# Attention weights summed over runs of four key tiles before their product with ones, and the last MLP's first weight loads written ahead of the residual stream's

## The chip, the cores and the metric

The kernel runs on one core of a Trainium2 chip. The core's engines work side by side, each with its own queue of instructions: TensorE (PE, matrix products; its weight loads are shown as PEld), VectorE (DVE), ScalarE (ACT), GpSimd (POOL) and SyncE (SP), on whose queue this kernel issues all of its transfers. They are kept in step by semaphores. The metric is the device time of one execution in microseconds: 3082.72 us is the median of three runs before the change (3080.58, 3082.72 and 3085.39).

## The reference

Two transformer layers in float32 on an input of 2 sequences x 1024 tokens x 512 features. Each layer adds an attention and an MLP, both on a layer norm, to the residual stream:

```python
x = x + _L0_attn_ref(_layernorm(x))   # gated delta rule, 6 heads of 64
x = x + _L0_ffn_ref(_layernorm(x))    # MLP, 4-bit weights, 512 -> 4096 -> 512
x = x + _L1_attn_ref(_layernorm(x))   # latent attention, 16 heads
x = x + _L1_ffn_ref(_layernorm(x))    # MLP, SiLU gate, 512 -> 2048 -> 512, two of every four kept
```

The change touches the third line and the passage into the fourth. The latent attention computes, for each of 16 heads (16 features for queries and keys, 32 for values),

```python
attn = jnp.einsum('bqhd,bkhd->bhqk', q, k) * scale
attn = jax.nn.softmax(attn, axis=-1)
out = jnp.einsum('bhqk,bkhd->bqhd', attn, v)
```

and multiplies the result by `wo`. The last MLP computes `silu(x @ w_gate) * (x @ w_up)`, keeps the two largest of each four in magnitude, and multiplies by `w_down`.

## The kernel before, in words

**The order of parts.** The work is laid out so that a part bound by small operations is woven with a part that keeps PE busy. `weave` (L157) takes steps from a main generator and, for each amount of time that it yields, takes filler steps of another. Three such weaves follow each other: the delta rule of sequence 1 beside the first MLP of sequence 0; the latent attention of sequence 0 beside the first MLP of sequence 1; and, the third part, `third()` (L2125), the latent attention of sequence 1 beside the last MLP of sequence 0 (`Sparse`, L1822). After that stands the last MLP of sequence 1 alone (`Sevens`, L1961), whose products are done with seven block products in place of eight, on sums of weight blocks that were made earlier and kept in HBM (`sums`). For PE, DVE, ACT and POOL the instructions are issued in the order in which the program writes them. SP's order is set by a scheduler.

**A value stage.** In `Latent.run` (L1461) queries are taken in two blocks of 512. For each block a score stage finds the largest score of every query, and a value stage, `values` (L1602), computes the weights again with keys as rows and sums the values. A value stage walks over 32 units: four groups of four heads, and in each group eight key tiles of 128 keys. In loop step `u` (L1703) it does:

- `weights(u)` (L1608): four matmuls, one for each head, to `st_ps` in PSUM; they lie in four row groups of the array and run side by side. ACT takes the exponential into two `es` tiles of 128 x 2 x 512, one for two heads; they come from a pool of eight.
- `gather(u - 1)` (L1639): four matmuls, in four column groups, add `es` times the values to `av_ps`.
- The sum of the exponentials over all keys, which divides the result. It goes through a product with a matrix of ones to `den_ps`, accumulated over the key tiles of a group. In the third part, for odd `u`, `pair(u)` (L1654) first adds the exponentials of key tile `u` onto those of `u - 1`: heads 0 to 2 on POOL, head 3 on DVE. Two steps later `total(u - 2)` (L1661) multiplies that pair's sum by ones, four matmuls.
- After the last key tile of a group, `oT` and `dn` are copied from PSUM, and `divide` (L1697) does four reciprocals and four products on DVE, up to three in a step.

An add onto `es[u - 1]` overwrites what `gather(u - 1)` reads, so POOL and DVE wait for that `av_ps` group. ACT writes a new `es` tile only where all readers of the one four units before are done. In the third part `per_value` is 0 (this is what `alone` stands for), so the weave hands out no steps of the MLP beside it during a value stage. In the second part (`running`) the sums go another way, on DVE alone, and the change leaves that as it is.

**The passage to the last MLP.** When the attention of sequence 1 is done, `third()` takes room for the residual stream of that sequence, `x_last`, and issues its eight loads (L2133). The rest of the MLP of sequence 0 follows. Then `Sevens` is constructed: it opens its pools and writes four sums of token blocks on DVE (`tokens`, L1972). Its `run` (L2024) issues the loads of the first two units of weights (`z_left`, each of three blocks of `w_gate` or `w_up` and one of `sums`), and starts.

Of the kernel before, what the change touches and what calls it, by code (L numbers as in the profile page):

```python
# [26 lines left out]
F32 = mybir.dt.float32  # L27
# [1384 lines left out]
class Latent:  # L1412
# [48 lines left out]
    def run(self, b, side, parked, out, per_score, per_value, running, beside=None, xT=None):  # L1461
# [140 lines left out]
        def values(q2, oT):  # L1602
# [5 lines left out]
            def weights(u):  # L1608
                gr, kt = units[u]
                tiles = [spot() for _ in range(2)]  # L1610
                for h4 in range(4):
                    r = 32 * h4
                    nc.tensor.matmul(  # L1613
                        tiles[h4 // 2][h4 % 2],
                        kT[r : r + CR, gr, kt * P : (kt + 1) * P],
                        q2[r : r + CR, gr, :],
                        start=True,
                        stop=True,
                    )
                es[u] = []  # L1620
                for tile in tiles:
                    t = two.tile([P, 2, QB], F32, tag="es", bufs=8 if alone else 6, name="es")
                    if len(tile) == 3:
                        nc.scalar.activation(t.rearrange("p i q -> p (i q)"), tile[2], AF.Exp, scale=HALF**-0.5)  # L1624
                    else:
                        for i in range(2):
                            nc.scalar.activation(t[:, i, :], tile[i], AF.Exp, scale=HALF**-0.5)
                    es[u].append(t)
# [22 lines left out]
                if kt == TT - 1:  # L1651
                    nc.vector.tensor_copy(oT[:, gr, :], av.pop(gr))

            def pair(u):  # L1654

                for h4 in range(4):
                    t = es[u - 1][h4 // 2][:, h4 % 2, :]
                    eng = nc.vector if alone and h4 == 3 else nc.gpsimd
                    eng.tensor_add(t, t, es[u][h4 // 2][:, h4 % 2, :])  # L1659

            def total(u):  # L1661
                gr, kt = units[u]
                if kt == 1:
                    den[gr] = banks.acc.tile([P, QB], F32, tag="den", name="den_ps")
                for h4 in range(4):
                    nc.tensor.matmul(  # L1666
                        den[gr][32 * h4 : 32 * h4 + 32, :],
                        self.ones,
                        es[u - 1][h4 // 2][:, h4 % 2, :],
                        start=(kt == 1),  # L1670
                        stop=(kt == TT - 1),
                    )
                if kt == TT - 1:
                    dn = two.tile([P, QB], F32, tag="dn", bufs=1, name="dn")
                    nc.vector.tensor_copy(dn, den.pop(gr))
                    for q in range(QT):
                        late.append(lambda q=q: divide(gr, q * P, dn, dn[:, q * P : (q + 1) * P]))
# [25 lines left out]
            for u in range(len(units) + 3):  # L1703
                if u < len(units):
                    weights(u)
                if 0 <= u - 1 < len(units):
                    gather(u - 1)
                if running:
                    if 0 <= u - 1 < len(units):
                        add(u - 1)  # L1710
                    if u > TT and u % TT == 1:
                        total_run(u // TT - 1)
                elif u % 2:
                    if u < len(units):
                        pair(u)
                    if u >= 3:
                        total(u - 2)
                yield per_value
                for _ in range(min(3, len(late))):
                    late.popleft()()  # L1720
# [240 lines left out]
class Sevens(Seven):  # L1961
# [3 lines left out]

    def __init__(self, core, banks, factors, xT, x, b, out):
        super().__init__(core, banks, AF.Silu, core.nc.vector)
        self.factors, self.x, self.b, self.out = factors, x, b, out
        self.wp = core.pools("z_w", 2)
        self.tmp = core.pools("z_tmp", 2)  # L1970
        self.one = core.pools("z_one")
        self.tokens(xT, self.one, core.nc.vector)  # L1972

    def close(self):
        self.core.pools.close("z_one", "z_tmp", "z_w")
# [46 lines left out]
            self.jobs.extend(((c, q), f) for f in calls)  # L2022

    def run(self):  # L2024
        self.left, wds = {}, {}
        todo = [(c, pair, w) for c in range(NC1) for pair in range(2) for w in ("gate", "up")]
        ws = {u: self.weights(u) for u in todo[:2]}

        def hidden(c):
            h = self.tmp.tile([P, 4, 2, T // 2], F32, tag="z_h", bufs=3, name="z_h")  # L2030
# [29 lines left out]
def two_layers(ctx, tc, a):  # L2060
# [25 lines left out]
    with tc.manual_schedule(engines={ENG.PE, ENG.DVE, ENG.Activation, ENG.Pool}):  # L2086
# [38 lines left out]
        def third():  # L2125
            xT = pools("xT_3").tile([P, KC, T], F32, name="xT3")
            done.append(xT)
            yield from att.run(1, None, parks[0], parks[1], 3.4, 0, False, xT=xT)
            x = pools("x3").tile([P, TT, DM], F32, name="x_last")
            held.append(x)  # L2130
            for n in range(TT, NT):
                core.x[n] = x[:, n - TT, :]
                nc.sync.dma_start(out=core.x[n], in_=parks[1][n])  # L2133

        held = []
        weave(third(), sparse.run(0, done[0], a["out"]))
        sparse.close()
        pools.close("xT_2", "x2", "l_w")

        sevens = Sevens(core, banks, factors, done[1], held[0], 1, a["out"])  # L2140
        sevens.run()
        sevens.close()
        pools.close("x3", "xT_3")


# [65 lines left out]
```

## Time and profile before

| | us |
|---|---|
| median of three runs | 3082.72 |
| lowest and highest run | 3080.58 and 3085.39 |
| the profiled execution | 3085.38 |
| its span in the trace | 3083.6 |
| PE busy | 3011.3 |
| DVE busy | 1909.1 |
| ACT busy | 960.7 |
| POOL busy | 695.6 |
| POOL's `es` adds (L1659), 96 | 132.6 |
| DVE's `es` adds (L1659), 32 | 41.3 |
| first value stage of the third part, from 2362.3 | 87.8 |
| second value stage of the third part, from 2640.8 | 95.3 |

Each of the 12652 matmuls counted is one of two records that one float32 product leaves. Matmuls that share the array run side by side, so the mean duration of one record (592 ns for `den_ps`) is not what a group of four products adds to PE's time: a group leaves eight records, and its length is read from the timeline. The granted clock of PE is 1.00 of full speed nearly everywhere; some short stretches have 0.50, and one of them covers 2645 to 2655 us, near the start of the second value stage.

### The profile page before, as it was taken

What the parts mean: (1) busy time and instruction counts of PE and PEld (TensorE: products, weight loads), DVE (VectorE), ACT (ScalarE), POOL (GpSimd) and SP (SyncE); (2) the same over time, 40 slices, a digit from 0 to 9 for tenths busy, and PEclk for the clock granted to TensorE, in tenths of its full rate; (3) what the DMA queues carried; (4) which work ended last, traced back from release to release, by engine and by line L of the source; (5) the groups of instructions that cost most, each with busy time, mean ns of one, the idle gap of its engine ahead of it and who ended that gap; (6) DMA issues with size and microseconds to landing.
All of it is one profiled execution on the core that took longest, in us unless ns stands there. A gap on an engine that the chain in (4) does not pass through costs nothing.

```text
span 3083.6 us, 35160 instructions
## 1 busy us (share of the span) xinstructions
PE 3011.3 (98%) x12652; PEld 1581.9 (51%) x12652; DVE 1909.1 (62%) x3554; ACT 960.7 (31%) x1488; POOL 695.6 (23%) x772
## 2 busy tenths in 40 slices
PE   7999999999999999999999999999999999999999
PEld 6777754555555554645435444446433243234547
DVE  6788733566666544477567656745675577364767
ACT  6554411222222211211462125522113510532221
POOL 3223102122222212464211221222002600440000
PEclk9999999999999999999999999999999999999999
DMA  4222313233232225155111110141010010025211
GB/s 139 66 82 69 90 55 110 67 98 101 96 96 80 90 93 171 58 190 194 36 50 64 52 62 26 36 147 59 24 41 1 32 52 14 1 75 164 72 48 52
DMA packets 196525, 235.36 MB, mean 76 GB/s; under 512 B 53952, under 2 KB 148672, under 8 KB 195840
## 3 DMA queue, kind: packets, MB, share of 16 engines
q1 hardware_dynamic: 196352, 233.12, 23.5%
q8 instruction: 100, 1.64, 0.2%
q14 instruction: 73, 0.60, 0.1%
HBM read 160.42 MB, written 72.61 MB: 76 GB/s over the span
## 4 chain that ended last, share of the span: by engine, by line
PE 81%; DVE 9%; DMA 2%; POOL 2%; issue 2%; ACT 1%; SPq 1%; DVEq 0%; POOLq 0%; ACTq 0%
PE z_ps L1042 24%; PE o_ps L201 12%; PE z_ps L1088 8%; PE u_ps L201 5%; PE g_ps L201 5%; PE st_ps L1613 5%; PE av_ps L1644 4%; PE s_ps L1555 4%; DVE cv L475 2%; DMA sums<-factor 1%; PE proj_ps L201 1%; DVE prod L617 1%; PE wide_ps L654 1%; PE small_ps L644 1%; PE den_ps L1666 1%
## 5 line engine op out<-in xcount | busy, mean ns | idle before, releaser
L1015 ACT COPY part<-z_ps 128x512 f32<-128x512 f32 x288 | 168.4, 585 | 712.8 <-PE z_ps L1042 506.0
L1042 PE MATMUL z_ps<-xT,z_left 128*128 128x512 f32 x768 | 361.1, 600 | 2.5 <-DMA z_left<-in_w_gate 2.4
L1564 DVE TENSOR_REDUCE top<-s_ps 128x2 f32<-128x1024 f32 x256 | 301.0, 1217 | 78.4 <-PE s_ps L1555 78.3
L1042 PE MATMUL z_ps<-xt,z_left 128*128 128x512 f32 x576 | 274.1, 598 | 1.2 <-DVE z_h L1060 1.0
L1624 ACT ACTIVATE es<-st_ps 128x1024 f32<-128x1024 f32 x214 | 209.9, 1023 | 126.0 <-PE st_ps L1613 120.8
L1042 PEld LDWEIGHTS z_ps<-xT,z_left 128*128 128x128 f32 x768 | 142.0, 191 | 189.7 <-issue 162.9
L201 PE MATMUL o_ps<-w_down,h 128*128 128x512 f32 x512 | 230.0, 598 | 0.6 <-DVE part L1076 0.6
L1042 PE MATMUL z_ps<-xT,w_left 128*128 128x512 f32 x384 | 179.5, 596 | 5.5 <-DVE h L1060 2.6
L1076 DVE TENSOR_TENSOR part<-z_ps,part 128x512 f32<-128x512 f32 x108 | 74.4, 689 | 178.6 <-PE z_ps L1042 172.9
L1042 PEld LDWEIGHTS z_ps<-xt,z_left 128*128 128x128 f32 x576 | 106.1, 190 | 145.5 <-issue 122.0
L1659 POOL TENSOR_TENSOR es<-es 128x512 f32<-128x512 f32 x96 | 132.6, 1408 | 143.8 <-PE av_ps L1644 140.1
L1613 PE MATMUL st_ps<-q,kT 17*128 17x512 f32 x1024 | 160.3, 649 | 1.7 <-ACT es L1624 1.7
L1555 PE MATMUL s_ps<-kT,q 16*128 16x512 f32 x1024 | 154.3, 640 | 4.6 <-DVE top L1564 4.6
L201 PEld LDWEIGHTS o_ps<-w_down,h 128*128 128x128 f32 x512 | 94.8, 191 | 108.1 <-issue 103.9
L201 PE MATMUL proj_ps<-xT,wqkv 128*128 128x256 f32 x576 | 133.1, 385 | 7.9 <-ACT raw L459 5.6
L1644 PE MATMUL av_ps<-es,v 128*32 128x512 f32 x1024 | 139.3, 615 | 0.0
L1042 PE MATMUL z_ps<-xt,w_left 128*128 128x512 f32 x288 | 136.4, 596 | 1.6 <-DVE part L1076 1.6
L1686 DVE TENSOR_TENSOR acc<-acc,es 128x1024 f32<-128x1024 f32 x96 | 130.6, 1408 | 0.0
L1077 POOL TENSOR_TENSOR h<-h,part 128x512 f32<-128x512 f32 x48 | 66.3, 1384 | 281.0 <-DVE part L1076 281.0
L1060 DVE TENSOR_TENSOR h<-z_ps,part 128x512 f32<-128x512 f32 x84 | 57.9, 689 | 103.7 <-PE z_ps L1042 91.4
L201 PEld LDWEIGHTS proj_ps<-xT,wqkv 128*128 128x128 f32 x576 | 108.0, 192 | 26.0 <-ACT raw L459 7.7
L1207 DVE TENSOR_TENSOR x<-x,o_ps 128x512 f32<-128x512 f32 x64 | 43.8, 684 | 120.0 <-PE o_ps L201 119.7
(317 smaller groups left out, 5167.3 us busy)
## 6 DMA issues: line engine op xcount, KB each, us to landing
sums<-factor SPq DMA_DIRECT2D x24, 512.0 KB, 3.2
kept_gate<-w_left SPq DMA_DIRECT2D x12, 896.0 KB, 3.8
kept_up<-w_left SPq DMA_DIRECT2D x12, 896.0 KB, 3.8
z_left<-kept_gate SPq DMA_DIRECT2D x12, 896.0 KB, 4.6
z_left<-kept_up SPq DMA_DIRECT2D x12, 896.0 KB, 4.5
wd<-kept_down SPq DMA_DIRECT2D x16, 512.0 KB, 4.5
xl<-park SPq DMA_DIRECT2D x32, 256.0 KB, 3.4
z_left<-sums SPq DMA_DIRECT2D x16, 512.0 KB, 4.1
```

The costliest lines, as they stand in the source:

```text
L201: nc.tensor.matmul(ps, lhsT, rhs, start=(i == 0), stop=(i == len(pairs) - 1))
L1015: self.core.nc.scalar.copy(t, src)
L1042: self.core.nc.tensor.matmul(ps, left[l][:, k, :], self.right[r][:, k, :], start=(first and k == 0), stop=(k == 1), skip_group_check=True,)
L1076: nc.vector.tensor_add(v, ps, v)
L1088: nc.tensor.matmul(ps[:, i * dm : (i + 1) * dm], left[l][:, k, i * P : (i + 1) * P], right[r][k], start=(first and i == 0 and k == 0), sto ...
L1555: nc.tensor.matmul(tiles[h4 // 2][:, h4 % 2 * 512 : h4 % 2 * 512 + 512], q1s[t][r : r + HALF, gr, :], kT[r : r + HALF, gr, j * 512 : (j + ...
L1564: nc.vector.tensor_reduce(top[:, j, h : h + 2], tiles[e].rearrange("p (i k) -> p i k", i=2), AX.X, ALU.max, negate=True)
L1613: nc.tensor.matmul(tiles[h4 // 2][h4 % 2], kT[r : r + CR, gr, kt * P : (kt + 1) * P], q2[r : r + CR, gr, :], start=True, stop=True,)
L1624: nc.scalar.activation(t.rearrange("p i q -> p (i q)"), tile[2], AF.Exp, scale=HALF**-0.5)
L1644: nc.tensor.matmul(av[gr][32 * h4 : 32 * h4 + 32, :], v[:, kt, 4 * gr + h4, :], es[u][h4 // 2][:, h4 % 2, :], start=(kt == 0), stop=(kt == ...
L1659: eng.tensor_add(t, t, es[u][h4 // 2][:, h4 % 2, :])
L1686: nc.vector.tensor_add(t, es[u - 1][e] if kt == 1 else t, es[u][e])
```

## The change

In the value stages of the third part, the exponentials of a run of four key tiles are summed on: each key tile but the first of a run is added onto the one before it, in place, so the fourth holds the sum of all four. `onto(u - 1)` does this in every loop step, and three steps later, once in four, `total(u - 3)` multiplies the fourth tile by ones. Which engines add which heads stays as it was. The pool of `es` tiles has ten in place of eight, which is five key tiles.

The second part moves two statements. `Sevens` is constructed in `third()`, between the making of the tile `x_last` and the issue of its loads; its constructor now issues the loads of the first two weight units, and the opening of the two other pools and the token sums have gone to the start of `run`.

```diff
-                    t = two.tile([P, 2, QB], F32, tag="es", bufs=8 if alone else 6, name="es")
+                    t = two.tile([P, 2, QB], F32, tag="es", bufs=10 if alone else 6, name="es")
...
-            def pair(u):
-
-                for h4 in range(4):
-                    t = es[u - 1][h4 // 2][:, h4 % 2, :]
-                    eng = nc.vector if alone and h4 == 3 else nc.gpsimd
-                    eng.tensor_add(t, t, es[u][h4 // 2][:, h4 % 2, :])
+            def onto(u):
+
+                if u % 4:
+                    for h4 in range(4):
+                        t, v = (es[i][h4 // 2][:, h4 % 2, :] for i in (u, u - 1))
+                        (nc.vector if h4 == 3 else nc.gpsimd).tensor_add(t, t, v)
 
             def total(u):
                 gr, kt = units[u]
-                if kt == 1:
+                if kt == 3:
                     den[gr] = banks.acc.tile([P, QB], F32, tag="den", name="den_ps")
                 for h4 in range(4):
                     nc.tensor.matmul(
                         den[gr][32 * h4 : 32 * h4 + 32, :],
                         self.ones,
-                        es[u - 1][h4 // 2][:, h4 % 2, :],
-                        start=(kt == 1),
+                        es[u][h4 // 2][:, h4 % 2, :],
+                        start=(kt == 3),
                         stop=(kt == TT - 1),
                     )
...
-                elif u % 2:
-                    if u < len(units):
-                        pair(u)
-                    if u >= 3:
-                        total(u - 2)
+                else:
+                    if 0 <= u - 1 < len(units):
+                        onto(u - 1)
+                    if u >= 6 and (u - 3) % 4 == 3:
+                        total(u - 3)
                 yield per_value
...
     def __init__(self, core, banks, factors, xT, x, b, out):
         super().__init__(core, banks, AF.Silu, core.nc.vector)
-        self.factors, self.x, self.b, self.out = factors, x, b, out
+        self.factors, self.x, self.b, self.out, self.xT = factors, x, b, out, xT
         self.wp = core.pools("z_w", 2)
-        self.tmp = core.pools("z_tmp", 2)
-        self.one = core.pools("z_one")
-        self.tokens(xT, self.one, core.nc.vector)
+        self.todo = [(c, pair, w) for c in range(NC1) for pair in range(2) for w in ("gate", "up")]
+        self.ws = {u: self.weights(u) for u in self.todo[:2]}
...
     def run(self):
-        self.left, wds = {}, {}
-        todo = [(c, pair, w) for c in range(NC1) for pair in range(2) for w in ("gate", "up")]
-        ws = {u: self.weights(u) for u in todo[:2]}
+        self.tmp = self.core.pools("z_tmp", 2)
+        self.one = self.core.pools("z_one")
+        self.tokens(self.xT, self.one, self.core.nc.vector)
+        self.left, wds, todo, ws = {}, {}, self.todo, self.ws
...
             x = pools("x3").tile([P, TT, DM], F32, name="x_last")
-            held.append(x)
+            sevens.append(Sevens(core, banks, factors, done[1], x, 1, a["out"]))
             for n in range(TT, NT):
                 core.x[n] = x[:, n - TT, :]
                 nc.sync.dma_start(out=core.x[n], in_=parks[1][n])
```

More of the change, by code (lines that the diff above doesn't have):

```diff
@@ L2133, in third @@
                 nc.sync.dma_start(out=core.x[n], in_=parks[1][n])
-        held = []
+        sevens = []
         weave(third(), sparse.run(0, done[0], a["out"]))
@@ L2138, in two_layers @@
         pools.close("xT_2", "x2", "l_w")
-        sevens = Sevens(core, banks, factors, done[1], held[0], 1, a["out"])
-        sevens.run()
-        sevens.close()
+        sevens[0].run()
+        sevens[0].close()
         pools.close("x3", "xT_3")
```

## The prediction

> **What bounds the kernel now.** The page's first part comes first:
>
> ```profile
> PE 3011.3 (98%) x12652; PEld 1581.9 (51%) x12652; DVE 1909.1 (62%) x3554; ACT 960.7 (31%) x1488; POOL 695.6 (23%) x772
> ```
>
> TensorE (PE) is busy nearly always, and POOL looks idle. That average says nothing about the two stretches that the change touches, the value stages of the third part. I found their ends in the timeline (first `st_ps` product to the first product after the last `den_ps` product) and cut them out with the table of busy times by stretch, together with one run of four key tiles inside the first:
>
> ```profile
> 2362.30:2450.10 87.80, 86.81 (x641) 24.18 (x640) 41.53 (x48) 64.14 (x86) 66.33 (x48) 1.00 0.00 1
> 2640.80:2736.10 95.30, 92.98 (x641) 24.72 (x640) 42.74 (x48) 65.44 (x87) 66.28 (x48) 0.93 0.00 1
> 2393.00:2403.50 10.50, 10.50 (x84) 2.96 (x80) 4.98 (x6) 7.91 (x11) 8.15 (x7) 1.00 0.01 2
> ```
>
> The columns after the length are PE, PEld, DVE, ACT, POOL, then the granted clock. In these stages POOL is busy 66.3 us of 87.8, three times its share of the whole. Four key tiles take 10.5 us, and POOL's six adds take about 8.2 of them. So PE is first, POOL a close second. The timeline of one pair of key tiles shows how they mesh:
>
> ```profile
> 2397.68 4.19 POOL L1659 TENSOR_TENSOR es<-es 128x512 f32<-128x512 f32 x3 [1.29 <-PE av_ps L1644]
> ...
> 2398.31 1.14 PE L1613 MATMUL st_ps<-q,kT 17*128 17x512 f32 x8
> 2398.38 1.12 DVE L1659 TENSOR_TENSOR es<-es 128x512 f32<-128x512 f32 x1 [1.45 <-ACT es L1624]
> ...
> 2399.38 1.06 PE L1644 MATMUL av_ps<-es,v 128*32 128x512 f32 x8
> ...
> 2400.38 1.39 PE L1613 MATMUL st_ps<-q,kT 17*128 17x512 f32 x8
> ...
> 2401.70 1.06 PE L1644 MATMUL av_ps<-es,v 128*32 128x512 f32 x8
> ...
> 2402.58 1.04 PE L1666 MATMUL den_ps<-es,ones 128*32 128x512 f32 x8
> ...
> 2402.92 4.19 POOL L1659 TENSOR_TENSOR es<-es 128x512 f32<-128x512 f32 x3 [1.06 <-PE av_ps L1644]
> ```
>
> Four heads' matmuls share the array, so one step's group (8 records) takes about 1.05 us whether it is `st_ps`, `av_ps` or `den_ps`. A pair is two groups of scores, two of values and one of sums: 5.25 us. POOL's three adds take 4.19 us, then POOL waits 1.06 us for the `av_ps` group that still reads the tile it will overwrite. Three adds cost more than three times the shortest add (1.257 us) because one of them, the one that DVE's add overlaps, takes 1.73 us.
>
> For the second part of the change, the passage into the last MLP:
>
> ```profile
> 2779.21 0.34 SPq L1844 DMA_DIRECT2D out<-x  x1
> 2779.60 1.48 SPq L1912 DMA_DIRECT2D z_left<-in_w_gate  x3
> ...
> 2782.78 5.40 PE L1042 MATMUL z_ps<-xT,z_left 128*128 128x512 f32 x8 [2.35 <-DMA z_left<-in_w_gate]
> ```
>
> PE idles 2.35 us there for the first weights, whose issue stands on SP's queue behind the eight `x_last` loads and the last output of the MLP before.
>
> **Part one, the sums, step by step.** Each stage has 32 key tiles, eight runs of four. Per run of four:
>
> PE: one `den_ps` group instead of two. Saved 1.04 us of 10.5, so PE needs about 9.46 us. Over 16 runs that is 16 x 1.04 = 16.6 us, if PE stays the bound.
>
> POOL: three key tiles are each summed onto the next, with three of four heads on POOL: nine adds instead of six. Three adds with a DVE add beside them take 4.18 us (4.17 to 4.20 in the timeline of both stages), and DVE again adds the fourth head, once per step. So 3 x 4.18 = 12.54 us. That is more than 9.46, and more than the 10.5 of today.
>
> DVE: three adds instead of two, 1.1 to 1.75 us each; it is busy 5 to 6.9 us of 10.5 today and stays below POOL.
>
> ACT: unchanged, 7.9 us of 10.5.
>
> POOL becomes the bound, if nothing makes it wait. I follow one period from the time E at which POOL ends the third sum of a run. PE then does the rest of `den_ps` (1.04). POOL skips one key tile and starts the next run's first sum at once, since that tile's `av_ps` group precedes the `den_ps` group in PE's order. The second sum needs the `av_ps` group two groups after `den_ps`, at about E + 3.2, and POOL is free at E + 4.18; the third needs the one at E + 5.3, against E + 8.36. The next `den_ps` group would be reached at E + 9.46 and waits for POOL until E + 12.54. With ten `es` tiles, that is five key tiles, ACT writes tile u + 5 into the place of u. The tightest is the tile freed at E + 8.36 by POOL's second next sum; it is wanted at about E + 8.4 and PE has 3 us to spare. DVE stands behind the `dn` copy once in eight key tiles until `den_ps` is done; its four reciprocals and products (0.95 + 0.3 to 0.9 each) and next two adds end before E + 10. Behind the waiting `den_ps` group on PE stand the next scores, so ACT idles with PE for these 3 us. So POOL never idles, and a stage is a start, 24 runs of three adds, and an end.
>
> First stage. POOL's first add waits for the second `av_ps` group instead of the first: that ends at 2368.78, and 0.12 us later POOL starts (as it did at 2366.83 after a group ending at 2366.71). 24 x 4.18 = 100.3, so POOL ends at 2469.2. Today the next part's first product stands 1.04 us behind POOL's last add (2449.10 to 2450.14), so 2470.25 against 2450.14: 20.1 us later.
>
> Second stage. The second `av_ps` group ends at 2652.23, so POOL ends at 2652.35 + 100.3 = 2752.7, the stage at 2753.7 against 2736.11: 17.6 us later. It is less because a half clock (0.50 from 2645 to 2655) has cost this stage some 7 us already, part of which falls where POOL will be the bound.
>
> Nothing hides this. `per_value` is 0 for this part, so no step of the MLP beside it is woven into a value stage, and what follows on PE stands in order behind the last `den_ps` group. The loads of `wo` and `xl`, which take the places of `es` tiles, wait for sums of the last key tiles and follow the stage's end as today; their first reader comes 10 us later (2736.29 to 2746.52). Sum: +37.7 us.
>
> How far may the price of a run of three adds be off? Below: adds that DVE does not disturb start 1.22 us apart in the timeline, 3.72 us for three, 89.3 us per stage; both stages together +15.7 us. Above: the only six adds back to back, 8.50 us at 2366.83, give 4.25, 102.0 us per stage, +41 us, and 0.1 us of waiting between runs would add 2.3 us a stage. I take 4.18, the nearest row: the same three adds with the same DVE add.
>
> A rule weighs against the change here and prices it otherwise. The Trainium skill, page "GPSIMD Engine Reference", section "Engine selection", puts an elementwise add of two tiles on VectorE, GpSimd being about two times slower; its section "Performance versus the Vector engine" has 4497 ns for 2048 elements. A quarter of that is 1.12 us, an estimate from the page, so nine adds would take 10.1 us and the period would shrink from 10.5 by 0.4 us: about 6 us faster over the 16. This trace's 1.39 us an add, with DVE beside it, decides.
>
> **Part two, the weights.** Their issue is written ahead of the eight `x_last` loads. In the built program SP's queue nevertheless keeps its order: eight loads, the last `out<-x`, then `z_left`. Two of these issues now also wait for PE, both for value-stage groups that end some 30 us before. So nothing is moved past anything, the right factors' four DVE sums stand where they stood, and the price is 0. Bounds: a gain of the whole 2.35 us if the weights came early; a loss of the 0.4 us of an issue slot.
>
> **Against the median.** The profiled execution took 3085.38 us, 2.66 us above the median of 3082.72. 3085.4 + 37.7 = 3123.1 stands for the first, 3120.4 for the second. An execution without the long half-clock stretch would lose 20.1 twice, 40.2. I forecast 3121.5.
>
> **Rivals.**
>
> *The clock falls as well.* PE will have 3 us of slack in every run of four. Today a wait of 1.54 us at 2642.86 comes just before the half clock, at which a group takes 1.94 us instead of 1.06. Were each second run half-clocked for the length of today's drop (2644 to 2658), PE would reach `den_ps` some 3.3 us after POOL is ready in two runs: 1.65 x 16 = 26 us more, 3147. Against: the end of each stage already is such a wait (`den_ps` groups trickling behind POOL's adds, idle for 0.2 and 0.6 us), and the clock kept 1.00 after both. The page "TensorE: Matmul & The Clock Gate", section "Part 1: The HAM clock gate", gates the clock after an idle window of about 3.4 us; by it the trickle would keep the clock. Here 1.54 us of waiting came before a drop.
>
> *PE stays the bound and the change is a gain.* If nine adds took less than 9.46 us, so 1.05 us an add or less, the 16.6 us would be won: 3066. The shortest of 96 adds took 1.257 us, which speaks against it. The point from which it decides against "slower" is 10.5 / 9 = 1.17 us an add.
>
> *The adds spread out.* DVE's add falls where POOL waits, and three adds cost 3.72 to 3.95: +16 to +27, 3099 to 3110. For it, runs beside DVE's reciprocals alone took 3.96 to 3.98 us. Against: DVE has one more add per run, POOL no pauses.
>
> *The weights do come early.* 2.35 us off, inside the range.
>
> **How the numbers follow.** A change of 0.2%, 6 us, is about what can be told from none. POOL bound at 4.0 to 4.3 us a run of three, 3112 to 3129: 0.76. Clock falls too, 3129 to 3150: 0.12. Adds spread out, 3098 to 3112: 0.07. Gain: 0.03, within 0.2%: 0.02. I set 3107 to 3138, which leaves out about half of the second case and part of the third.
>
> **What would show it.** Right: `es` adds on POOL 144 with a mean near 1.39 us and hardly any wait for `av_ps`; POOL busy about 100 us in each stage; `den_ps` records halved to 128, waiting for `es` adds of POOL in every run; stages of some 108 us; the 2.35 us before the last MLP unchanged. Wrong: POOL idle inside the stages, adds near 1.25 us, or a clock well below 1.00 in both stages.

## The result, and the profile after

The changed kernel took 3121.64 us, the median of four runs (3116.78 to 3124.35), against 3081.89 us for the kernel before beside it: a ratio of 1.0125 (95% interval 1.0109 to 1.0141). It is slower by about 40 us, as forecast. The profiled execution took 3120.2 us, with a span of 3118.5 us.

The first part of the page of the changed kernel, busy time by engine:

```profile
PE 3027.7 (97%) x12524; PEld 1573.4 (50%) x12524; DVE 1942.3 (62%) x3570; ACT 961.5 (31%) x1488; POOL 764.1 (25%) x820
```

128 matmul records are gone, 48 POOL instructions and 16 DVE instructions have come, and no share looks alarming. PE is counted busy for 16 us more with fewer products: groups are drawn out, as shown below, and more of the second stage ran at half clock. Next, the table of busy times by stretch for the two value stages of the changed kernel; after the length come PE, PEld, DVE, ACT and POOL, then the granted clock:

```profile
2355.50:2463.90 108.40, 96.58 (x581) 22.55 (x580) 57.51 (x56) 64.31 (x86) 99.97 (x72) 0.98 0.05 16
2654.60:2771.00 116.40, 105.29 (x578) 23.44 (x577) 58.54 (x56) 65.59 (x87) 99.95 (x72) 0.88 0.04 12
```

POOL has gone from 66.3 to 100.0 us in each, and the stages from 87.8 to 108.3 and from 95.3 to 116.4 us (measured, as before, from the first `st_ps` product to the first product after the last `den_ps` product). The timeline of POOL alone, over both stages, says it most plainly:

```profile
2362.10 99.97 POOL L1659 TENSOR_TENSOR es<-es 128x512 f32<-128x512 f32 x72 [35.17 <-PE av_ps L1644]
```

```profile
2666.03 12.42 POOL L1659 TENSOR_TENSOR es<-es 128x512 f32<-128x512 f32 x9 [78.21 <-PE av_ps L1644]
2681.57 87.54 POOL L1659 TENSOR_TENSOR es<-es 128x512 f32<-128x512 f32 x63 [3.13 <-PE av_ps L1644]
```

In the first stage POOL does its 72 adds in one unbroken line: 99.97 us, or 4.165 for three. In the second it does the nine of the first run, stands 3.13 us, and does the other 63. The end of one run of four key tiles of the changed kernel, seen from PE and DVE:

```profile
2393.75 1.77 DVE L1659 TENSOR_TENSOR es<-es 128x512 f32<-128x512 f32 x1
...
2396.17 1.07 PE L1644 MATMUL av_ps<-es,v 128*32 128x512 f32 x8
...
2396.70 0.11 PEld L1666 LDWEIGHTS den_ps<-es,ones 128*32 128x32 f32 x1 [0.38 <-POOL es L1659]
2396.72 3.43 DVE L1659 TENSOR_TENSOR es<-es 128x512 f32<-128x512 f32 x2
2397.05 1.98 PE L1666 MATMUL den_ps<-es,ones 128*32 128x512 f32 x4
...
2399.66 1.05 PE L1666 MATMUL den_ps<-es,ones 128*32 128x512 f32 x4 [0.62 <-POOL es L1659]
2400.64 0.31 PEld L1613 LDWEIGHTS st_ps<-q,kT 17*128 17x128 f32 x8 [0.84 <-issue]
```

The `den_ps` group, which used to take 1.04 us, is spread over 3.6 us (2397.05 to 2400.64), because its products wait one after the other for POOL's adds. The groups of adds in these stages (the three numbers after x144 are the shortest, the median and the longest add in ns), and then what the users of the `den_ps` tile waited for, as us and times:

```profile
L1659 POOL TENSOR_TENSOR es<-es x144: 1252/1298/1740, 2362.1 to 2767.9; 128x512 f32<-128x512 f32 x144
...
L1659 DVE TENSOR_TENSOR es<-es x48: 810/1723/1808, 2362.2 to 2762.8; 128x512 f32<-128x512 f32 x48
```

```profile
  POOL es L1659: 79.8, 72
  PE den_ps L1666: 27.3, 8
```

The first row is PE waiting for POOL's adds, the second DVE's copy of `den_ps` waiting for PE. Before, the same list had 13.8 us in 30 waits for POOL.

The passage into the last MLP of the changed kernel, from the timeline:

```profile
2814.09 0.34 SPq L1844 DMA_DIRECT2D out<-x  x1
2814.53 1.44 SPq L1912 DMA_DIRECT2D z_left<-in_w_gate  x3
...
2817.59 0.30 PEld L1042 LDWEIGHTS z_ps<-xT,z_left 128*128 128x128 f32 x2 [2.53 <-DMA z_left<-in_w_gate]
2817.59 4.97 PE L1042 MATMUL z_ps<-xT,z_left 128*128 128x512 f32 x7 [2.29 <-DMA z_left<-in_w_gate]
```

The loads of `z_left` still stand behind the last output, and PE still waits 2.29 us.

Span against span: the stages are 20.5 and 21.1 us longer, and everything ahead of the first stage was 6.8 us shorter in this execution (it had 20.5 us at half clock there, the other 34.1). 41.7 - 6.8 = 34.9 us, which is 3118.5 - 3083.6.

### The profile page after: what moved, and what is told of

The parts are those of the page before. It is cut to its first block, busy times and chain, and to the rows that moved or that the text cites. A ratio compares the mean times of both kernels' runs of the same rounds, so it can differ in the third digit from the quotient of the medians.

```text
span 3118.5 us, 35023 instructions
## 1 busy us (share of the span) xinstructions
PE 3027.7 (97%) x12524; PEld 1573.4 (50%) x12524; DVE 1942.3 (62%) x3570; ACT 961.5 (31%) x1488; POOL 764.1 (25%) x820
## 4 chain that ended last, share of the span: by engine, by line
PE 80%; DVE 10%; POOL 3%; issue 3%; DMA 1%; ACT 1%; SPq 0%; DVEq 0%; POOLq 0%; ACTq 0%
PE z_ps L1042 25%; PE o_ps L201 12%; PE z_ps L1088 8%; PE u_ps L201 5%; PE g_ps L201 5%; PE st_ps L1613 5%; PE s_ps L1555 4%; PE av_ps L1644 4%; DVE cv L475 2%; POOL es L1659 1%; DVE prod L617 1%; PE proj_ps L201 1%; PE wide_ps L654 1%; PE small_ps L644 1%; DVE inv L618 1%
## 5 line engine op out<-in xcount | busy, mean ns | idle before, releaser
L1659 POOL TENSOR_TENSOR es<-es 128x512 f32<-128x512 f32 x144 | 199.9, 1428 | 116.5 <-PE av_ps L1644 116.5
```

What stands on the lines that cost most here:

```text
L1659: (nc.vector if h4 == 3 else nc.gpsimd).tensor_add(t, t, v)
```

## The experiments

The diffs are against the changed kernel, where nothing else is said. A stage's length is always from its first `st_ps` product to the first product after its last `den_ps` product, in the profiled execution, the first stage named first.

**1 and 2. Each part of the change alone.** First the sums alone, with `Sevens` as it was:

```diff
-            sevens.append(Sevens(core, banks, factors, done[1], x, 1, a["out"]))
+            held.append(x)
...
+        sevens = Sevens(core, banks, factors, done[1], held[0], 1, a["out"])
```

> The sums over four key tiles alone; Sevens is built and loads its weights where it did before the change. Theory (POOL's nine adds in a run of four are the bound, and the moved loads cost and bring nothing): as the whole change, 3121 us within 3, value stages of 108 us and 108 to 117 us. Rival (the moved loads, or the waits for PE that two of them got, cost time): 3118 us or less.

Measured: 3122.29 us, ratio 1.0121 (1.0106 to 1.0137), stages of 108.2 and 116.4 us. Then the loads alone, against the kernel before:

```diff
-        self.tmp = core.pools("z_tmp", 2)
-        self.one = core.pools("z_one")
-        self.tokens(xT, self.one, core.nc.vector)
+        self.todo = [(c, pair, w) for c in range(NC1) for pair in range(2) for w in ("gate", "up")]
+        self.ws = {u: self.weights(u) for u in self.todo[:2]}
```

> The moved loads alone, the sums of pairs as before the change. Theory (SP's order is the same, so nothing moves): 3082 us within 3, and PE waits 2.3 to 2.6 us for the first z_left as before. Rival (the weights come early): that wait gone and 2.4 us less; which is below what the times can tell, so the wait itself is read.

Measured: 3084.57 us against 3085.75, ratio 0.9996 (0.9987 to 1.0006), stages of 87.8 and 95.2 us. So the whole loss is the sums', and the second part is worth nothing that these times can tell, as its unchanged place on SP's queue said. The wait for the first `z_left` was 1.66 us here, outside the 2.3 to 2.6 that I had expected. It does not follow the move: with the sums alone (experiment 1), where the loads stand where they did, it was 1.87 us.

**3. The product with ones one step later.**

```diff
-                    t = two.tile([P, 2, QB], F32, tag="es", bufs=10 if alone else 6, name="es")
+                    t = two.tile([P, 2, QB], F32, tag="es", bufs=11 if alone else 6, name="es")
...
-            for u in range(len(units) + 3):
+            for u in range(len(units) + (3 if running else 4)):
...
-                    if u >= 6 and (u - 3) % 4 == 3:
-                        total(u - 3)
+                    if u >= 7 and (u - 4) % 4 == 3:
+                        total(u - 4)
```

> The changed kernel with the product with ones one step of the loop later (of key tile u-4 in place of u-3), with one more buffer pair's half for the exponentials (11 in place of 10) and one step more at the end. The work of every engine is the same. Theory (GpSimd's nine additions per run set the pace, so that waiting longer before the product brings nothing): 3121 us, stages of 107 to 109 and 115 to 119 us. Rival (the product merely stands too early and the additions would fit if they were given a step more): stages fall by some 3 us per run of four, the kernel to 3100 us or less.

Measured: 3124.78 us, ratio 1.0141 (1.0126 to 1.0155), stages of 108.3 and 116.4 us. The product does not merely stand too early: waiting longer changes nothing, which is what one expects where POOL's adds set the pace.

**4. A second head on VectorE.**

```diff
-                        (nc.vector if h4 == 3 else nc.gpsimd).tensor_add(t, t, v)
+                        (nc.vector if h4 >= 2 else nc.gpsimd).tensor_add(t, t, v)
```

> The change with head 2 added on VectorE as well, so POOL has six adds in a run of four and VectorE six. Theory (POOL's adds are the bound, one that VectorE's add overlaps 0.46 us longer): 6 x 1.24 + 6 x 0.46 = 10.2 us for a run of four, stages of about 89 us, 3082 to 3087 us. Rival (VectorE's own adds, 1.72 us in the trace of the change, become the bound): 6 x 1.72 + 3.2 = 13.5 us for a run of four, 3135 us. Rival (the place of the product with ones in PE's order, not POOL's rate, makes PE wait): no change from 3121 us.

Measured: 3104.93 us, ratio 1.0072 (1.0048 to 1.0096), stages of 100.1 and 108.9 us. Two thirds of POOL's adds gave half of what I expected. The groups of adds of this kernel, and the table by stretch for its first stage:

```profile
L1659 DVE TENSOR_TENSOR es<-es x96: 677/1127/1771, 2363.0 to 2752.6; 128x512 f32<-128x512 f32 x96
L1659 POOL TENSOR_TENSOR es<-es x96: 1265/1716/1803, 2363.0 to 2753.8; 128x512 f32<-128x512 f32 x96
```

```profile
2356.41:2456.47 100.06, 88.59 (x577) 22.05 (x576) 80.56 (x80) 64.31 (x86) 73.75 (x48) 0.99 0.05 16
```

POOL's median add rose from 1298 to 1716 ns: now most of them have a DVE add beside them. But POOL's rate is not why the stage missed its 89 us. POOL was busy for 73.8 us, less than the 81.6 that my price makes (eight runs of 10.2), and idle for the rest of the 100.1. PE's `den_ps` products now waited longer for DVE's adds (37.2 us in both stages) than for POOL's (23.4). So POOL was no longer the bound, and DVE's queue, with six adds of a run and the reciprocals in it, held the products back.

**5. Six adds on POOL, three on VectorE.** The kernel leaves out the sum of the third head (the ones product reads the first head's in its place), which takes a third of POOL's work away and gives DVE nothing:

```diff
-                    for h4 in range(4):
+                    for h4 in (0, 1, 3):
                         t, v = (es[i][h4 // 2][:, h4 % 2, :] for i in (u, u - 1))
...
-                        es[u][h4 // 2][:, h4 % 2, :],
+                        es[u][(0, 0, 0, 1)[h4]][:, (0, 1, 1, 1)[h4], :],
```

> The change without the adds of head 2, whose sum is left out: the product with ones reads head 0's sum for it. POOL has six adds in a run of four, VectorE three. Theory (POOL's rate): 8.4 us of POOL under PE's 9.46, so PE is the bound and the saving of the product with ones shows: stages of about 79.5 us, 3082 - 16.6 = 3065 us. Rival (place of the product with ones, or a clock that falls because of the waits): above 3075 us.

Measured: 3098.21 us, ratio 1.0043 (1.0028 to 1.0058), stages of 90.5 and 101.9 us. It is faster than the change, so POOL's adds were the bound; but it doesn't reach what PE alone would allow. Its timeline shows where the rest stands:

```profile
2397.40 0.94 DVE L1700 RECIPROCAL dn<-dn 128x128 f32<-128x128 f32 x1
...
2398.37 0.29 DVE L1701 TENSOR_TENSOR oT<-oT,dn 128x128 f32<-128x128 f32 x1
...
2398.58 3.43 DVE L1659 TENSOR_TENSOR es<-es 128x512 f32<-128x512 f32 x2
2400.39 0.14 PEld L1666 LDWEIGHTS den_ps<-es,ones 128*32 128x32 f32 x2 [2.21 <-DVE es L1659]
2400.39 1.04 PE L1666 MATMUL den_ps<-es,ones 128*32 128x512 f32 x2 [1.30 <-DVE es L1659]
```

The copy of `den_ps` and the reciprocals and products of the group before stand ahead of DVE's adds, which then take 1.75 us each beside POOL's. `den_ps` waited 22.9 us for DVE and 15.6 us for POOL in the two stages. So this is the wait of experiment 4 again, with fewer adds. Besides, half clock covered 23.9 us of the second stage, as in the changed kernel.

**6. No adds on VectorE.** Here the fourth head is left out of the sums in the same way (the ones product reads the third head's), and POOL keeps its nine adds:

```diff
-                    for h4 in range(4):
+                    for h4 in (0, 1, 2):
...
-                        es[u][h4 // 2][:, h4 % 2, :],
+                        es[u][(0, 0, 1, 1)[h4]][:, (0, 1, 0, 0)[h4], :],
```

> The changed kernel with VectorE's own addition left out (the fourth head's exponentials are not summed on, the product with ones reads the third head's sum in their place), so that GpSimd does its nine additions per run of four key tiles with no VectorE addition beside them. Theory (the two engines slow each other down: a GpSimd addition started 1.22 to 1.24 us apart where VectorE was not adding and 1.7 us where it was): GpSimd's run of four key tiles falls from 12.54 to about 9 x 1.24 = 11.2 us, each value stage from 108 to about 98 us, and the kernel lands near 3101 us (3097 to 3106), with GpSimd's mean addition at 1.25 us. Rival (an addition costs GpSimd 1.39 us by itself, whatever VectorE does): 3121 us, as the changed kernel.

Measured: 3132.55 us, ratio 1.0155 (1.0129 to 1.0181), stages of 108.1 and 117.8 us. The adds did what the theory said, and the stages did not get shorter. The timelines of POOL and of DVE in this kernel show why:

```profile
2389.05 24.60 POOL L1659 TENSOR_TENSOR es<-es 128x512 f32<-128x512 f32 x20
2423.97 3.73 POOL L1659 TENSOR_TENSOR es<-es 128x512 f32<-128x512 f32 x3 [10.32 <-PE av_ps L1644]
```

```profile
2394.44 19.36 DVE L1701 TENSOR_TENSOR oT<-oT,dn 128x128 f32<-128x128 f32 x1
2413.73 0.94 DVE L1700 RECIPROCAL dn<-dn 128x128 f32<-128x128 f32 x1
...
2417.29 0.68 DVE L1652 COPY oT<-av_ps 128x512 f32<-128x512 f32 x1
2418.03 0.20 PEld L1644 LDWEIGHTS av_ps<-es,v 128*32 128x32 f32 x8 [9.65 <-DVE oT L1652]
```

POOL's twenty adds, the last of an unbroken line of 36, take 1.23 us each, as expected without DVE's. But one product of DVE, 128x128 with both operands in SBUF, which takes 0.29 us elsewhere, lasted 19.36 us and ended at 2413.80, 0.15 us after the last of these adds. Behind it stood the copy of `av_ps`, behind that copy PE (9.65 us), and behind PE POOL, which had run dry. The same happened at 2728.88 (19.36 us) and 2449.81 (19.35 us), each time ending 0.15 us after the last add of an unbroken line. So the theory on the price of an add held (median 1276 ns, 177.7 us for 144 in place of 199.9), and in the first stage a new wait of 10.3 us on POOL ate all of the gain. It does not account for a kernel that is 11 us slower than the changed one: in the profiled executions this one is 14.1 us longer, and all but 1.1 us of that lies outside the stages: 7.3 ahead of the first, where the two programs are the same, 3.9 between the two and 1.8 behind them. The granted clock was 0.980 to 0.986 in the four executions, against 0.989 to 0.991 for the changed kernel; whether the held products brought the clock down is not shown.

**7. All adds on VectorE.** One instruction for two heads, POOL none:

```diff
-                    for h4 in range(4):
-                        t, v = (es[i][h4 // 2][:, h4 % 2, :] for i in (u, u - 1))
-                        (nc.vector if h4 == 3 else nc.gpsimd).tensor_add(t, t, v)
+                    for t, v in zip(es[u], es[u - 1]):
+                        nc.vector.tensor_add(t, t, v)
```

> The changed kernel with every addition on VectorE, as one instruction of 128x1024 for a pair of heads (six in a run of four key tiles), and none on GpSimd. Theory (VectorE's addition of 512 takes 0.68 us when GpSimd does not add beside it): six additions of about 1.25 us and the copies, reciprocals and products of 3.2 us make about 10.7 us per run, so stages of 88 to 94 us and a kernel between 3083 and 3096 us. Rival (the 1.1 to 1.7 us that its additions took in the changed kernel and its variants are VectorE's own price): six of 2.2 us and 3.2 us make 16.4 us per run, stages of some 135 us, 3170 us.

Measured: 3100.32 us, ratio 1.0061 (1.0041 to 1.008), stages of 93.1 and 101.9 us. The group of these adds:

```profile
L1658 DVE TENSOR_TENSOR es<-es x96: 1215/1219/1227, 2364.7 to 2743.3; 128x1024 f32<-128x1024 f32 x96
```

With POOL silent an add of 1024 takes 1.22 us, each time. So 0.61 us for each 512 is DVE's own price (its shortest add of 512 in experiment 4 took 0.68), and the 1.72 us of the changed kernel were POOL's doing. The time is 4 us above my range: the first stage fits (88 to 94), the second one again had 23.9 us at half clock.

**8 and 9. Runs of three, three and two, and the product a step later.** Ten adds and three ones products in eight key tiles, all adds on DVE. Against the kernel of experiment 7:

```diff
-                if u % 4:
+                if u % 8 % 3:
...
-                if kt == 3:
+                if kt == 2:
                     den[gr] = banks.acc.tile([P, QB], F32, tag="den", name="den_ps")
...
-                    if u >= 6 and (u - 3) % 4 == 3:
+                    if u >= 5 and (u - 3) % 8 in (2, 5, 7):
                         total(u - 3)
```

> Every addition on VectorE as 128x1024, and runs of three, three and two key tiles in place of four and four: ten additions and three products with ones per eight key tiles. Theory (TensorE is the bound where nobody adds for longer than it multiplies): VectorE has 10 x 1.25 + 6.4 = 18.9 us per eight key tiles, TensorE 21.0 - 1.05 = 19.95 us; stages of 82 to 86 us in place of 87.8 and 95.3 of the kernel before, the second one more for its stretch at half clock, so 3068 to 3080 us, below the kernel before. Rival (VectorE's queue, in which a copy that waits for the last product with ones and four reciprocals and products stand ahead of additions, holds the next product back, as where two heads' additions were left to it): each group of 32 key tiles loses some 3 us four times in a stage, stages of 96 us, 3085 to 3100 us.

Measured: 3089.04 us, ratio 1.002 (1.0011 to 1.003), stages of 89.5 and 97.2 us: the time is the rival's, at the mild end of its price. The next kernel differs from this one only in that the product stands a step later:

```diff
-                    if u >= 5 and (u - 3) % 8 in (2, 5, 7):
-                        total(u - 3)
+                    if u >= 6 and (u - 4) % 8 in (2, 5, 7):
+                        total(u - 4)
```

> Every addition on VectorE as 128x1024, runs of three, three and two key tiles, and the product with ones one step later (of key tile u-4 in place of u-3). Theory (VectorE has 18.9 us of work for eight key tiles beside TensorE's 19.95 us, and the 13.6 us that the products waited for its additions in the first stage are an order of its queue, four reciprocals and products ahead of two additions, which a step of 2.1 to 2.3 us more hides): the first stage falls from 89.5 to 81 to 84 us; in the second one the half clock, which ends with the first product, lasts one window longer (20.5 in place of 17.0 us), 89 to 93 us; the kernel 3077 to 3083 us. Rival (VectorE's rate is the limit): 89 and 98 us, 3089 us.

Measured: 3076.17 us (3064.11 to 3082.29), ratio 0.9975 (0.9959 to 0.9991), both stages of 83.5 us in the profiled execution. The stretches of the two kernels, first stage of each:

```profile
2360.40:2449.90 89.50, 85.97 (x613) 21.63 (x612) 65.33 (x72) 64.20 (x86) 0.00 (x0) 1.00 0.02 4
```

```profile
2360.50:2444.00 83.50, 82.35 (x611) 21.12 (x610) 65.21 (x72) 64.39 (x86) 0.00 (x0) 1.00 0.01 2
```

With the same work on every engine, a step more of distance took 6.0 us out of the stage: here the bound was the order of DVE's queue, not its rate (65.2 us busy). The `den_ps` products waited 5.6 us for DVE's adds in that stage, in place of 13.6. This is the counterpart of experiment 3, where the same step was worth nothing because POOL had no time to spare. Three of the nine executions took 3064 to 3067 us at a granted clock of 0.995 or 0.996, the profiled one (3066.76) among them; six took 3075 to 3082 us at 0.988 to 0.991. So the second stage of 83.5 us, all of it at full clock, need not hold for the six.

**10. One more ones product early in each stage.** The changed kernel, with an added ones product of the first key tile in the third step; the first proper one overwrites its result:

```diff
-                if kt == 3:
+                if kt == (3 if gr else 0):
                     den[gr] = banks.acc.tile([P, QB], F32, tag="den", name="den_ps")
...
-                        start=(kt == 3),
-                        stop=(kt == TT - 1),
+                        start=(kt in (0, 3)),
+                        stop=(kt in (0, TT - 1)),
...
-                    if u >= 6 and (u - 3) % 4 == 3:
-                        total(u - 3)
+                    if u == 2 or u >= 6 and (u - 3) % 4 == 3:
+                        total(max(u - 3, 0))
```

> The changed kernel with one product with ones more, of the first key tile's exponentials at the third step of each value stage; its result is overwritten by the first proper product. It changes no addition. Theory (the half clock at the start of the second value stage lasts until the first product with ones runs: in the kernel before and after and in the variant with six GpSimd additions it ended in the 3.41 us window of the first one, after 13.6, 23.9 and 23.9 us): the stretch ends in the window of the added product, after some 3.4 to 7 us in place of 23.9; the first stage stays at 108 us, the second falls from 116.4 to about 110 us, and the kernel to about 3116 us. Rival (the stretch's length has another cause, such as the rate of the key tiles): it stays at 20 to 24 us, the second stage at 116 us, the kernel at 3121 us.

Measured: 3121.65 us, ratio 1.0129 (1.0107 to 1.0151). The half clock at the start of the second stage lasted 10.2 us in place of 23.9 and ended in the stretch in which the added product ran (2669.95 to 2671.9), which PE reached later than I had thought. The second stage fell to 112.87 us, 3.5 us less. Medians of four runs that spread over 13 us don't show that.

**11. The same, sooner, in the kernel before.** Against that kernel; the product takes the values of the first key tile, which are ready long before:

```diff
-                if kt == 1:
+                if kt == 1 and gr:
                     den[gr] = banks.acc.tile([P, QB], F32, tag="den", name="den_ps")
...
+                if u == 1 and not running:
+                    den[0] = banks.acc.tile([P, QB], F32, tag="den", name="den_ps")
+                    for r in range(0, P, 32):
+                        nc.tensor.matmul(den[0][r : r + 32, :], self.ones, v[:, 0], start=True, stop=True)
                 if 0 <= u - 1 < len(units):
                     gather(u - 1)
```

> The kernel before with one product with ones more in each value stage, of the value tile of the first key tile (ready long before), ahead of the first product with values, in the place where TensorE waits for ScalarE's first exponentials; its result is overwritten. Theory (the half clock of 13.6 us at the start of the second value stage lasts until a product with ones runs): it does not come, or ends within one or two windows (3.4 to 6.8 us); the second stage falls from 95.3 to 88.5 to 92 us, the kernel to 3076 to 3080 us. Rival (the clock is released by something else that comes with the first proper product): 13.6 us at half clock as before, 3082 to 3084 us.

Measured: 3085.13 us against 3082.40, ratio 1.0006 (0.9995 to 1.0016). The half clock fell from 13.6 to 6.8 us, and the second stage from 95.3 to 93.4 us, less than I had expected; the first stage grew by 0.9 us, and 1.6 us came between the stages. The half clock moved, and the time did not.

**12. Both: experiment 9 with the early product of experiment 11.**

> Both: all additions on VectorE in runs of three, three and two with the product one step later, and the extra product ahead of the first product with values in each value stage. If both theories hold, the two stages take 81 to 85 us each, and the kernel 3066 to 3074 us, below the kernel before. If only the one on the clock holds, 89 and 90 us, 3081 to 3084 us; if only the one on VectorE's queue holds, 3077 to 3083 us.

Measured: 3068.69 us (3067.13 to 3070.68), ratio 0.9956 (0.9944 to 0.9968), stages of 86.0 and 84.4 us, the first a microsecond above what I expected. It beats both kernels, the one before by 13.7 us:

```profile
2362.20:2448.20 86.00, 84.84 (x620) 21.55 (x620) 65.22 (x72) 64.39 (x86) 0.00 (x0) 0.98 0.01 2
2638.80:2723.20 84.40, 83.25 (x618) 21.39 (x617) 65.22 (x72) 64.39 (x86) 0.00 (x0) 1.00 0.01 2
```

PE is busy for all but about 1.2 us of each stage: it is the bound again, with one ones product fewer in eight key tiles. What the early product adds to this is not shown: the first stage is 2.5 us longer than in experiment 9, with the clock at half for 3.4 us of it, and the second stage ran at full clock in the profiled execution of experiment 9 as well, without that product. The last section says what the two executions share.

## Why the prediction was right, point by point

**The bound.** "POOL becomes the bound" and "the same three adds with the same DVE add" at 4.18 us: 72 adds took 99.97 us, 4.165 for three, against 100.3 forecast. That is 1.39 us an add, as named; the mean record has 1428 ns, because the records overlap. The price rests on the two engines disturbing each other: experiment 6 took DVE's 48 adds away, and POOL's 144 got 22.2 us cheaper, 0.46 for each DVE add. The page "SBUF — State Buffer" of the Trainium skill, section "SBUF: two separate sides", describes the port pair that DVE and GpSimd share as an exclusive lock that the later one waits for when DVE reads two operands from SBUF. The durations here agree that the two wait for each other: POOL's shortest add took 1.25 us, and 1.7 where DVE's fell beside it; DVE's shortest took 0.68 us in experiments 4 and 5, its median one in the changed kernel 1.72.

**The first stage.** Forecast +20.1 us, measured +20.5. POOL started 6.57 us into the stage (forecast 6.56). The end was 0.8 us longer than forecast: 1.8 us passed from POOL's last add to the next part's first product in place of 1.04; the clock had fallen to 0.50 for the last 3.4 us of the stage.

**The second stage.** Forecast +17.6, measured +21.1. The step that was mis-sized is "So POOL never idles", which holds at full clock. POOL's line broke for 3.13 us after the ninth add, because PE was still at half clock and hadn't made the next key tiles. I had taken the half clock as it was before, 13.6 us; it lasted 23.9. The change itself brought this about, as far as experiments 10 and 11 show: with runs of four the first ones product comes 26.7 us into the stage in place of 15.1, and the half clock lasted until then. The table by stretch of the changed kernel, at 3.4 us a row (the last four of it):

```profile
2671.90:2675.30 3.40, 3.40 (x16) 0.56 (x12) 1.00 (x1) 1.93 (x3) 3.40 (x3) 0.50 0.00 0
2675.30:2678.70 3.40, 3.40 (x20) 0.72 (x16) 0.00 (x0) 2.00 (x3) 3.15 (x3) 0.50 0.02 5
2678.70:2682.10 3.40, 3.40 (x24) 0.60 (x16) 0.44 (x1) 1.94 (x2) 0.53 (x1) 0.50 0.00 0
2682.10:2685.50 3.40, 3.40 (x31) 1.07 (x24) 1.80 (x2) 1.60 (x3) 3.40 (x3) 0.99 0.00 0
```

POOL runs dry in the third row (0.53 us busy of 3.40). The other 0.8 us of the miss are the stage's end, at half clock as in the first stage, less 0.3 that the adds were cheaper. Experiment 10 took the gap away: with the half clock cut to 10.2 us POOL's line in the second stage is unbroken, and the stage took 112.87 us, which is what the forecast's 95.3 + 17.6 makes:

```profile
2670.31 99.92 POOL L1659 TENSOR_TENSOR es<-es 128x512 f32<-128x512 f32 x72 [78.29 <-PE av_ps L1644]
```

This is a weak form of the rival "the clock falls as well": in one place, some 3 us, not in each run.

**The waits inside the stages.** The prediction gave PE 3 us of slack in every run and took it that the clock would keep 1.00 over them. It did, but for the start of the second stage and one stretch of 3.4 us at the end of each.

**DVE "stays below POOL".** True of the change (57.5 us busy of 108.4) and correct as to its order: the next `den_ps` group waited for POOL 72 times and, in that list, never for DVE. But it was close. As soon as POOL's load fell by a third (experiments 4 and 5), DVE's order was in the way. The rival "PE stays the bound" was priced as if only POOL's rate stood against it; experiments 4, 5 and 7 say that a faster POOL would not have brought 3066 us.

**Part two.** Price 0: measured -1.2 us with an interval that holds 0 (experiment 2), and in the changed kernel the wait is 2.29 us after 2.35. Nothing was lost or won there in the profiled executions either: from the end of the second stage to the end of the span it is 347.5 us before and after.

**The sum.** Forecast 3121.5, measured 3121.64 us. That is closer than its terms were: the second stage was 3.5 us too low and the first 0.4, and the executions of this kernel spread over 7.6 us for what lies outside both. The mechanism was right; that the sum came within 0.2 us is luck.

## What to carry to other kernels

Saving TensorE a product by summing ahead moves work to an engine that may have less time to spare: price the run on each engine, and on VectorE and GpSimd with the other one's adds beside them, and look at what else stands in the queue of the engine that gets the work (experiment 4). When a product waits for sums, try it a step later; if nothing changes, a rate is the bound (experiment 3), and if it helps, an order was (experiment 9). And try VectorE alone where it has the time: it did the same runs of four 21 us faster than the split of nine adds and three.

## What the runs showed of the hardware that was not expected

**A line of GpSimd adds can hold a VectorE instruction for as long as it lasts.** In experiment 6, three products of 0.29 us lasted 19.36, 19.36 and 19.35 us, through some fifteen POOL adds, and ended 0.15 us after the line did. The page cited above speaks of a lock held for one instruction. In the changed kernel, whose line of 72 adds has no gap either, the longest such product took 0.95 us. That DVE adds as well there is not the difference: in experiment 6 itself the four products from 2706.54 on fell beside an unbroken line of 45 adds and took 0.96, 0.39, 0.39 and 0.40 us, and a later one beside the same line (2728.88) was held. What decides it stays open.

**At half clock, TensorE stayed there while fully busy, until a product with ones ran.** The half clock at the start of the second stage began 2.9 to 3.7 us after the stage's start, in all profiled executions but those of experiments 9 and 12. While it lasted, PE did only `st_ps` and `av_ps` groups until the first `den_ps` group. Its length followed the first `den_ps` product:

| kernel | first ones product | half clock ended | length |
|---|---|---|---|
| before, early product (11) | 2643.07 | 2648.0 | 6.8 |
| changed, one more product (10) | 2669.95 | 2672.1 | 10.2 |
| before | 2655.89 | 2657.7 | 13.6 |
| loads alone (2) | 2652.33 | 2653.9 | 13.6 |
| runs of 3, 3, 2 (8) | 2662.56 | 2662.8 | 17.0 |
| changed | 2681.22 | 2682.2 | 23.9 |
| sums alone (1) | 2684.88 | 2685.7 | 23.9 |
| two heads on VectorE (4) | 2673.08 | 2675.3 | 23.9 |
| six POOL adds (5) | 2670.67 | 2673.3 | 23.9 |
| none on VectorE (6) | 2692.2 | 2692.9 | 23.9 |
| all on VectorE (7) | 2668.0 | 2670.9 | 23.9 |
| ones product later (3) | 2692.3 | 2692.8 | 27.3 |

The page "TensorE: Matmul & The Clock Gate", section "Part 1: The HAM clock gate", has the full clock come back after one busy window of about 3.4 us. In the changed kernel PE was busy for 3.40 us of each of six such stretches in a row, and none brought it back; the first two rows of the table by stretch above are two of them. That adding a product shortens the stretch is shown (10 and 11, one profiled execution each). Why it does is not, and in experiment 8 only 0.3 us of the product lay before the clock rose. Nor does the wait of 1.54 us for the first exponentials explain the drop, as the prediction hinted: in the kernels of experiments 4, 5, 7 and 8 that wait was 0.21 us, and the clock fell all the same, while in the profiled executions of 9 and 12, with the same 0.21 us, the second stage ran at full clock throughout.

**Whether the clock falls there goes with where a fixed step of 3.41 us lies.** Within each trace all changes of the granted clock are whole multiples of 3.413 us apart; in the changed kernel it falls at 2658.27, rises at 2682.16 (7 steps later), falls at 2767.50 (25) and rises at 2770.91 (1). Count these steps through all 28 value stages of the 14 traces. In 13 of them a step ends 2.9 to 3.7 us after the stage's start, and in each of the 13 the clock falls at that moment. In the other 15 it ends 1.1 to 2.8 us after the start, and in none does the clock fall there. The second stages of experiments 9 and 12 belong to the 15 (2.15 and 2.78 us); the first stage of experiment 12 (2.96 us) belongs to the 13, and its clock fell in spite of the early product. In the second stage of experiment 12 that product began 3.3 us into the stage, later than the moment at which the clock might have fallen. So the full clock there is not the early product's doing, as far as these traces show; it goes with the place of the step, which no experiment here set. The rise follows the same steps: in 11 of the 12 rows of the table it came at the end of the step in which the first ones product began, and in experiment 11 one step later. What in a step decides is not shown. The other executions of experiment 9 and those of experiment 12 were not traced, so their second stages are not known.
